# One stage of two dense graph layers, or two stages on neighbouring graphs

## The chip, the cores and the metric

The kernel runs on one core of one Trainium2 chip. The metric is the device time of one launch in microseconds; the figure for a kernel is the median of its runs. One execution is recorded by the hardware profiler.

The engines have short names in the profile: PE is TensorE (matmuls and transposes), DVE is VectorE, ACT is ScalarE, POOL is GpSimd, which here issues the indirect gathers, and SP issues nearly all other DMAs. Each engine works through its own list of instructions in order, and waits on semaphores for the others.

## The reference, cut to what matters

Sixteen graphs of 1024 nodes with 64 features each, an adjacency matrix of 1024 x 1024 floats per graph, and four layers, each of the form x + layer(relu(layernorm(x))):

```
h = max(layernorm(x), 0);  x = x + L0(h, adj)   # two-layer MLP, relu(A @ m), then a GRU cell
h = max(layernorm(x), 0);  x = x + L1(h, adj)   # (h * dinv) summed over neighbours, @ kernel, relu
h = max(layernorm(x), 0);  x = x + L2(h, adj)   # thin the neighbours, weighted quantiles of them, MLP
h = max(layernorm(x), 0);  x = x + L3(h, adj)   # (A + I) @ h, divided by the row sums
```

Layers 0, 1 and 3 multiply by the whole adjacency matrix. Layer 2 instead needs, for every node and feature, quantiles over that node's neighbours. The kernel makes lists of neighbours, gathers their rows of the table h and sorts them. The lists depend on the adjacency alone; the gathers need the table, which is the output of layers 0 and 1.

## The kernel before, in words

**Stages of a graph.** Lines 1852 to 1858 make, for every graph b, twelve Python generators: `fetch` and `load` (the adjacency is fetched, transposed on PE and stored as adjT in DRAM), `code`, `rank`, `cut` and `list` (the lists of neighbours, ending in the indices idxH and idxL), `mid` (layers 0 and 1 and the norm ahead of layer 2, dense01, line 1328), `gath` (POOL's gathers: 28 for the 128 nodes with the longest lists, "heavy", and 54 for all others, "light", in two groups), `sort` (heavy sorts on VectorE), `smalls` (light sorts), `sums`, and `rear` (the end of layer 2 and layer 3, dense23).

**What orders the work.** The program is not a loop. The class Order (line 209) keeps a model clock for each engine; `run` (line 241) resumes, again and again, the stage whose next piece can start earliest, and on a tie the one that stands first in the list of stages. What a stage issues when resumed goes at the end of its engines' instruction lists. The list is sorted by the dictionary `first` (line 1859): rear, sums and gath, then mid, list, cut, rank and code, then load and fetch, and the sorts last; within one rank by graph, so an older graph comes first. A stage can wait for another through `after(...)`: `middle` (line 1806) waits for mid of the graph before; `gathers` (line 1811) for its own list and its own mid, and for the last graph's gathers; `loads` (line 1768) for the rear stage DEPTH graphs back, since adjT, the table and other DRAM buffers exist DEPTH times (line 677).

**Buffers.** A tile name or tag has a number of buffers; a new tile with a tag waits, on the chip, for the readers of the old one. X, the running features of the graph in mid, has one buffer (line 1329), the norm's output hm has one, and the [128, 1024] tiles m1T, rz, g0 and g1 share the one buffer "big".

**Layer by layer in mid.** X is fetched; layernorm_relu (line 1226) takes a reduction on VectorE, eight squares with accumulation and a square root on ScalarE, three small VectorE steps, and eight scaled relus on ScalarE. The MLP follows (transposes, product, second product), then `propagated` (line 1288): sixteen matmuls of 512 columns against adjT, whose eight row blocks `streamed` (line 1275) brings in as tiles am of 512 KB, three buffers for all users. The stage that streams is put at the head of the list of stages. The GRU follows with sigmoid and tanh on ScalarE, and X is updated (line 1391, the instruction X<-X,hm). Then layer 1: row scales dinv, the norm into tr, the propagation, the product with wk, the transposition back and the scaling into u1, X updated again (X<-X,u), stored as x1 for the rear stage, normed once more (hm) and stored as the table tab (line 1422).

**Two PSUM pools** serve all stages: four tiles "bank" and two tiles "bank2"; a propagation holds a bank2 from its first matmul to its eviction.

Of the kernel before, what the change touches and what calls it, by code (L numbers as in the profile page):

```python
# [18 lines left out]
P = 128  # L19
EPS = 1e-5  # L20
STRIP = 1
DEPTH = 5
LIGHTBUFS = (2, 1)
HB = 2
SGN = 2
# [386 lines left out]
def kernel(  # L412
# [117 lines left out]
    def lists_for_all():  # L530
# [694 lines left out]

        def layernorm_relu(X, h=None, who="m", times=None):

            yield "V", X
            s = wp.tile([P, NT], F32, name="ln_s", bufs=2)
            V.reduce_sum(s, X, AX.X)  # L1230
            V.tensor_scalar(s, s, -1.0 / H, None, ALU.mult)
            yield "A", s
            v = wp.tile([P, NT], F32, name="ln_v", bufs=2)
            if h is None:
                h = wp.tile([P, NT, H], F32, name="h" + who, tag="h2r" if who == "r" else None, bufs=1)
            for t in range(NT):
                A.activation(h[:, t, :], X[:, t, :], AF.Square, bias=s[:, t : t + 1], accum_out=v[:, t : t + 1])
            A.activation(v, v, AF.Sqrt, bias=eps, scale=1.0 / H)
            yield "V", v
            V.reciprocal(v, v)  # L1240
            if times is not None:
                V.tensor_mul(v, v, times)
            V.tensor_mul(s, s, v)
            yield "A", s, v
            for t in range(NT):
                A.activation(h[:, t, :], X[:, t, :], AF.Relu, bias=s[:, t : t + 1], scale=v[:, t : t + 1])
            return h
# [6 lines left out]
        def t2(name, who="m"):  # L1254
            return wp.tile([P, NT, H], F32, name=name, tag="t2" + who, bufs=1)
# [69 lines left out]
                pm.append(q)  # L1325
            return pm

        def dense01(b, S):
            X = wp.tile([P, NT, H], F32, name="X", bufs=1)
            S_.dma_start(X, x[b].rearrange("(t p) h -> p t h", p=P))  # L1330

            h = yield from layernorm_relu(X)
            cat = wp.tile([P, N], F32, name="cat")
            yield from transposed(h, cat[0:H, :])
            yield "T", cat
            m1T = wp.tile([P, N], F32, name="m1T", tag="big")
            pm = yield from product(w1, cat[0:H])
            yield from evicted(pm, m1T[0:H], AF.Relu, b1)
            yield "T", m1T
            yield after(f"load{b}")  # L1340
            p2 = yield from bank()
            T.matmul(p2, *bias(0), start=True, stop=False)
            ams = streamed(b, 0)
            for t in range(NT):
                o = p2[:, t * H : (t + 1) * H]
                T.matmul(o, m1T[0:H, t * P : (t + 1) * P], w2, start=False, stop=t == NT - 1)
            yield "A", p2
            A.activation(m2x[:, :, 0:H], p2.rearrange("p (t h) -> p t h", h=H), AF.Relu)
            ps1.close(p2)
            pm = yield from propagated(b, m2x, 0, ams)  # L1350

            yield "A", pm
            A.copy(m1T[H : H + 1, :], pm[H : H + 1, :])
            yield from evicted(pm, cat[H:P], AF.Relu)
            yield "T", m1T
            pr = yield from bank()
            for t in range(NT):
                T.transpose(
                    pr[:, t : t + 1], m1T[H : H + 1, t * P : (t + 1) * P], ident[H : H + 1, H : H + 1]
                )  # L1360
            yield "V", pr
            S["rs"] = rs = st.tile([P, NT], F32, name="rs")
            V.tensor_scalar(rs, pr[:, 0:NT], 1.0, None, ALU.add)
            ps1.close(pr)
            rz = wp.tile([P, NT, 2 * H], F32, name="rz", tag="big")
            nn = t2("nn")
            for g in range(2):
                yield "T", cat
                pg = yield from bank2()
                for i in range(4):  # L1370
                    t = 4 * g + i
                    o = pg[:, i * 4 * H : (i + 1) * 4 * H]
                    if i % 2 == 0:
                        T.matmul(pg[:, i * 4 * H : (i + 2) * 4 * H], *bias(2), start=True, stop=False)
                    T.matmul(o, cat[:, t * P : (t + 1) * P], wg, start=False, stop=i % 2 == 1)
                pgv = pg.rearrange("p (i c) -> p i c", c=4 * H)
                gs = slice(4 * g, 4 * g + 4)
                yield "A", pg
                A.activation(rz[:, gs, :], pgv[:, :, 0 : 2 * H], AF.Sigmoid)
                yield "V", rz  # L1380
                V.tensor_mul(nn[:, gs, :], pgv[:, :, 2 * H : G], rz[:, gs, 0:H])
                V.tensor_add(nn[:, gs, :], nn[:, gs, :], pgv[:, :, G : 4 * H])
                ps2.close(pg)
            yield "A", nn
            A.activation(nn, nn, AF.Tanh)
            yield "V", nn

            V.tensor_sub(h, h, nn)
            V.tensor_mul(h, h, rz[:, :, H : 2 * H])
            V.tensor_add(h, h, nn)  # L1390
            V.tensor_add(X, X, h)

            ams = streamed(b, 1)

            dinv = wp.tile([P, NT], F32, name="dinv", bufs=2)
            V.tensor_scalar(dinv, rs, 1e-30, None, ALU.max)
            yield "A", dinv
            A.activation(dinv, dinv, AF.Sqrt)
            yield "V", dinv
            V.reciprocal(dinv, dinv)  # L1400
            V.scalar_tensor_tensor(dinv, rs, 0.0, dinv, ALU.is_gt, ALU.mult)
            tr = yield from layernorm_relu(X, t2("tr"), "m", dinv)
            pm = yield from propagated(b, tr, 1, ams, own=True)
            g0 = wp.tile([P, N], F32, name="g0", tag="big")
            yield from evicted(pm, g0[0:H])
            yield "T", g0
            pm = yield from product(wk, g0[0:H])
            g1 = wp.tile([P, N], F32, name="g1", tag="big")
            yield from evicted(pm, g1[0:H])
            pa = yield from back(g1[0:H])  # L1410
            yield "A", pa
            u1 = t2("u1")
            scaled(u1, pa, dinv, AF.Relu)
            ps1.close(pa)
            yield "V", u1
            V.tensor_add(X, X, u1)

            yield "S", X
            S_.dma_start(D[b % DEPTH]["x1"].rearrange("(t p) h -> p t h", p=P), X)
            h2 = yield from layernorm_relu(X)  # L1420
            yield "S", h2
            S_.dma_start(D[b % DEPTH]["tab"][1 : N + 1, :].rearrange("(t p) h -> p t h", p=P), h2)

# [75 lines left out]
        def sort_heavy(b, S):  # L1499
# [92 lines left out]
            yield ("V",)  # L1592

            agh = qp.tile([P, 64], F32, name="agh", bufs=2)
            split = qp.tile([P, 320], F32, name="split", bufs=1)
            pair = kept = 0
            for _, nr, q, bf, where in KEPT:
                n = nr // 4
                wv = wb[:, kept : kept + nr // 2 * q].rearrange("p (a i s) -> p a i s", i=2, s=q)
                v, k0 = None, 0  # L1600
                if len(where) > 1:
                    v = split[:, 0 : nr // 2 * q].rearrange("p (a s i) -> p a i s", i=2, s=q)
                for first, st_, k in where:
                    w = hb[bf]
                    ap = [list(z) for z in w.ap]
# [159 lines left out]
        def after(*names):  # L1765
            return lambda: all(n in order.done for n in names)
# [39 lines left out]
        def middle(b, S):  # L1806
            if b:
                yield after(f"mid{b - 1}")
            yield from dense01(b, S)

        def gathers(b, S):
            yield after(f"list{b}", f"mid{b}")
            if b:
                yield after(f"gath{b - 1}")
            if b >= HB:
                yield after(f"heavy{b - HB}")
            yield from gather_heavy(b, S)
            yield f"gh{b}"
            for g in range(len(NETS)):
                if b >= LIGHTBUFS[g]:  # L1820
                    yield after(f"sum{b - LIGHTBUFS[g]}.{g}")
                yield from gather_light(b, S, g)
                yield f"gl{b}.{g}"
# [28 lines left out]
        for b in range(B):  # L1852
            S = {}
            for name, stage in (
                ("rear", rear), ("mid", middle), ("fetch", fetching), ("load", loads), ("code", coding), ("rank", ranking), ("cut", cutting), ("list", listing),
                ("gath", gathers), ("sort", sorts), ("smalls", light_sorts), ("sums", sums),
            ):
                order.add(f"{name}{b}", stage(b, S))
        first = {"rear": 0, "sums": 0, "gath": 0, "conv": 1, "mid": 1, "list": 1, "cut": 1, "rank": 1, "code": 1, "load": 2, "fetch": 2, "sort": 7, "smalls": 7}
        order.stages.sort(key=lambda q: first[q[0].rstrip("0123456789")])  # L1860
        with tc.manual_schedule():
            order.run()
# [383 lines left out]
```

## Time and profile before

| what | us |
|---|---|
| median of three runs | 2694.49 |
| the three runs | 2689.75 to 2709.9 |
| the profiled execution | 2692.04 |
| its span, first to last instruction | 2690.2 |
| mean granted clock of TensorE | 0.769 of full |

How to read the profile: nearly every instruction carries the line L406, since the helper class Engine issues them all there; so instructions are told apart by the tiles that they write and read, "out<-in", with numbers left out. A row of a group reads: line, engine, operation, tiles, count, then busy time and mean length in ns, then the idle time of that engine just before these instructions and what ended most of it. A row of a timeline reads: start, length, engine, operation, tiles, count, and in brackets idle time before it and what ended it. A row of a view by stretches gives the stretch, its length, the busy time and instruction count of PE, its weight loads (PEld), DVE, ACT and POOL, the granted clock, and the busy share of the DMA engines with GB/s. A row of waits reads: who waited for whom, us in total, times, the longest.

### The profile page before, as it was taken

The numbers are of one execution on the slowest core, as the hardware profiler recorded it, in microseconds if no ns is written. First come the engines' busy times: TensorE is split into PE (matmuls) and PEld (weight loads), VectorE is DVE, ScalarE is ACT, GpSimd is POOL, SyncE is SP. The second block draws the span as 40 slices with busy tenths as digits, with TensorE's granted clock in tenths as the row PEclk, the third lists the DMA queues.
The fourth block names the chain that finished last, engine by engine and source line by source line (L and its number), as shares of the span: only waits on it lengthen the run. The fifth ranks groups of instructions, "written<-read, shape, count | busy, mean of one in ns | idle before, by whom it ended". The sixth has DMA issues, their size and how long they took to land.

```text
span 2690.2 us, 35021 instructions
## 1 busy us (share of the span) xinstructions
PE 1855.6 (69%) x9250; PEld 976.0 (36%) x9250; DVE 2034.3 (76%) x6403; ACT 1650.2 (61%) x5062; POOL 1590.3 (59%) x1502
## 2 busy tenths in 40 slices
PE   5866777678877667776777758688676757675314
PEld 3433444334343333434433334344333423232102
DVE  3448879986967969679893977979599694968581
ACT  8567876856575864778647676675767555353312
POOL 4037367776647674475746837476574745767761
PEclk7867787787868689686887859788686977877566
DMA  7546656565566556473656627475563644444322
GB/s 223 171 133 200 192 157 185 155 186 167 157 179 175 152 155 189 130 245 97 190 156 172 217 69 215 156 213 146 170 206 88 182 136 124 142 118 142 75 56 83
DMA packets 388338, 423.93 MB, mean 158 GB/s; under 512 B 160668, under 2 KB 297442, under 8 KB 388130
## 3 DMA queue, kind: packets, MB, share of 16 engines
q1 hardware_dynamic: 340610, 374.10, 44.1%
q0 software_dynamic: 47520, 47.51, 9.4%
q8 instruction: 76, 1.25, 0.2%
q14 instruction: 132, 1.08, 0.1%
HBM read 337.08 MB, written 84.37 MB: 157 GB/s over the span
## 4 chain that ended last, share of the span: by engine, by line
DVE 35%; PE 25%; ACT 15%; DMA 10%; POOL 6%; issue 5%; SPq 3%; DVEq 0%; ACTq 0%; POOLq 0%
PE bank L406 25%; DVE hb L406 12%; DMA am<-adjT 6%; DVE s L406 5%; POOL s L406 5%; DVE o L406 4%; SPq L406 3%; ACT sgn L406 2%; ACT hm L406 2%; DVE ln_s L406 1%; ACT u L406 1%; ACT s L406 1%; ACT junk L406 1%; DMA s<-tab,idxL 1%; ACT strip L406 1%
## 5 line engine op out<-in xcount | busy, mean ns | idle before, releaser
L406 POOL DMA_INDIRECT s<-tab,idxL x864 | 980.0, 1134 | 263.4 <-issue 257.9
L406 POOL DMA_INDIRECT gh<-tab,idxH x448 | 457.1, 1020 | 694.7 <-PE bank L406 174.8
L406 DVE TENSOR_TENSOR hb<-hb 128x128 f32<-128x128 f32 (+10 forms) x1040 | 520.9, 535 | 41.9 <-ACT hb L406 37.2
L406 PE MATMUL bank<-am,tr 128*64 128x512 f32 x512 | 281.7, 692 | 114.9 <-ACT tr L406 50.2
L406 PE MATMUL bank<-am,hr 128*64 128x512 f32 x512 | 265.2, 656 | 72.5 <-DMA am<-adjT 38.7
L406 PE MATMUL bank<-am,m2x 128*65 128x512 f32 x512 | 260.0, 648 | 35.4 <-DMA am<-adjT 34.2
L406 PE MATMUL bank<-ident,a 128*128 128x128 f32 x1024 | 192.2, 332 | 43.9 <-DMA a<-in_adj_dram 14.2
L406 ACT COPY strip<-bank 128x512 f32<-128x512 f32 x256 | 144.3, 586 | 90.5 <-PE bank L406 84.5
L406 ACT ACTIVATE s<-s,wl 128x64 f32<-128x64 f32 x704 | 188.6, 342 | 17.6 <-DVE s L406 17.6
L406 POOL DMA_INDIRECT zz<-agg,posi x128 | 125.6, 981 | 91.4 <-issue 37.0
L406 DVE TENSOR_TENSOR hb<-hb,hb 128x488 f32<-128x488 f32 (+7 forms) x368 | 173.2, 484 | 5.0
L406 PEld LDWEIGHTS bank<-am,tr 128*64 128x64 f32 x512 | 74.6, 157 | 277.1 <-issue 148.2
L406 PEld LDWEIGHTS bank<-ident,a 128*128 128x128 f32 x1024 | 141.0, 169 | 94.0 <-issue 29.8
L406 PE MATMUL bank<-cx,oh 128*128 128x133 f16 (+1 forms) x1280 | 144.1, 262 | 25.9 <-DVE oh L406 18.9
L406 ACT ACTIVATE g<-bank 64x512 f32<-64x512 f32 x96 | 51.9, 586 | 168.5 <-PE bank L406 168.5
L406 PEld LDWEIGHTS bank<-am,hr 128*64 128x64 f32 x512 | 70.0, 149 | 228.4 <-issue 135.1
L406 DVE TENSOR_TENSOR o<-s 128x1152 f32<-128x1152 f32 (+2 forms) x192 | 139.8, 751 | 17.1 <-DMA s<-tab,idxL 16.0
L406 ACT ACTIVATE sgn<-strip 128x1024 bf16<-128x1024 f32 x128 | 135.2, 1056 | 18.8 <-issue 9.6
L406 ACT ACTIVATE junk<-bank,nkey 128x1024 bf16<-128x1024 f32 x128 | 141.2, 1117 | 5.5 <-PE bank L406 5.5
L406 DVE TENSOR_TENSOR s<-s 128x128 f32<-128x128 f32 (+5 forms) x272 | 104.1, 398 | 52.9 <-ACT s L406 49.9
L406 DVE TENSOR_TENSOR s<-s,o 128x576 f32<-128x576 f32 (+5 forms) x256 | 138.0, 547 | 2.4
L406 ACT ACTIVATE sgn<-sgn 128x1024 bf16<-128x1024 bf16 x128 | 135.3, 1057 | 4.1
(399 smaller groups left out, 3986.0 us busy)
## 6 DMA issues: line engine op xcount, KB each, us to landing
am<-adjT SPq DMA_DIRECT2D x384, 512.0 KB
a<-in_adj_dram SPq DMA_DIRECT2D x128, 512.0 KB
adjT<-strip SPq DMA_DIRECT2D x128, 512.0 KB
s<-tab,idxL POOLq DMA_INDIRECT x864
gh<-tab,idxH POOLq DMA_INDIRECT x448
wb<-wd SPq DMA_DIRECT2D x32, 196.0 KB
X<-in_x_dram SPq DMA_DIRECT2D x16, 256.0 KB
x<-X SPq DMA_DIRECT2D x16, 256.0 KB
```

What stands on the lines that cost most here:

```text
L406: return f(*args, **kw)
```

## The change

dense01 is cut after the GRU. The first part, dense0, stays in the stage `mid`; the second, dense1, becomes a stage `next` with rank 1 in `first`, as mid has, and placed before mid of the same graph. `next` of graph b waits for mid of b and next of b-1; `mid` of graph b waits for mid of b-1 and for next of b-2; the gathers wait for next instead of mid. X gets two buffers. The second part gets its own buffers: tiles with the tag "t2n", h2 (before in the buffer of hm) among them, "bign" of 64 rows for g0 and g1, and ln_s and ln_v by stage. DEPTH goes from 5 to 6. The tile `split` (320 columns) that the heavy stage's weighting used is dropped; the front of the buffer hb[1] takes its place.

```
-DEPTH = 5
+DEPTH = 6
...
-            s = wp.tile([P, NT], F32, name="ln_s", bufs=2)
+            s = wp.tile([P, NT], F32, name="ln_s" + who, bufs=2)
...
-            v = wp.tile([P, NT], F32, name="ln_v", bufs=2)
+            v = wp.tile([P, NT], F32, name="ln_v" + who, bufs=2)
...
-        def dense01(b, S):
-            X = wp.tile([P, NT, H], F32, name="X", bufs=1)
+        def dense0(b, S):
+            S["X"] = X = wp.tile([P, NT, H], F32, name="X", bufs=2)
             S_.dma_start(X, x[b].rearrange("(t p) h -> p t h", p=P))
...
             V.tensor_add(X, X, h)
 
+        def dense1(b, S):
+            X, rs = S["X"], S["rs"]
             ams = streamed(b, 1)
...
-            tr = yield from layernorm_relu(X, t2("tr"), "m", dinv)
+            tr = yield from layernorm_relu(X, t2("tr", "n"), "n", dinv)
             pm = yield from propagated(b, tr, 1, ams, own=True)
-            g0 = wp.tile([P, N], F32, name="g0", tag="big")
-            yield from evicted(pm, g0[0:H])
+            g0 = wp.tile([H, N], F32, name="g0", tag="bign")
+            yield from evicted(pm, g0)
...
-            u1 = t2("u1")
+            u1 = t2("u1", "n")
...
-            h2 = yield from layernorm_relu(X)
+            h2 = yield from layernorm_relu(X, t2("h2", "n"), "n")
...
-            split = qp.tile([P, 320], F32, name="split", bufs=1)
...
-                    v = split[:, 0 : nr // 2 * q].rearrange("p (a s i) -> p a i s", i=2, s=q)
+                    v = hb[1][:, 0 : nr // 2 * q].rearrange("p (a s i) -> p a i s", i=2, s=q)
...
         def middle(b, S):
             if b:
                 yield after(f"mid{b - 1}")
-            yield from dense01(b, S)
+            if b >= 2:
+                yield after(f"next{b - 2}")
+            yield from dense0(b, S)
+
+        def second(b, S):
+            yield after(f"mid{b}")
+            if b:
+                yield after(f"next{b - 1}")
+            yield from dense1(b, S)
 
         def gathers(b, S):
-            yield after(f"list{b}", f"mid{b}")
+            yield after(f"list{b}", f"next{b}")
...
-                ("rear", rear), ("mid", middle), ("fetch", fetching), ("load", loads), ("code", coding), ...
+                ("rear", rear), ("next", second), ("mid", middle), ("fetch", fetching), ("load", loads), ("code", coding), ...
...
-        first = {"rear": 0, "sums": 0, "gath": 0, "conv": 1, "mid": 1, ...}
+        first = {"rear": 0, "sums": 0, "gath": 0, "next": 1, "mid": 1, ...}
```

More of the change, by code (lines that the diff above doesn't have):

```diff
@@ L1401, in dense01 @@
             V.scalar_tensor_tensor(dinv, rs, 0.0, dinv, ALU.is_gt, ALU.mult)
-            tr = yield from layernorm_relu(X, t2("tr"), "m", dinv)
+            tr = yield from layernorm_relu(X, t2("tr", "n"), "n", dinv)
             pm = yield from propagated(b, tr, 1, ams, own=True)
-            g0 = wp.tile([P, N], F32, name="g0", tag="big")
-            yield from evicted(pm, g0[0:H])
+            g0 = wp.tile([H, N], F32, name="g0", tag="bign")
+            yield from evicted(pm, g0)
             yield "T", g0
[L1407 to L1410, printed above, removed]
+            pm = yield from product(wk, g0)
+            g1 = wp.tile([H, N], F32, name="g1", tag="bign")
+            yield from evicted(pm, g1)
+            pa = yield from back(g1)
             yield "A", pa
-            u1 = t2("u1")
+            u1 = t2("u1", "n")
             scaled(u1, pa, dinv, AF.Relu)
@@ L1854, in lists_for_all @@
             for name, stage in (
-                ("rear", rear), ("mid", middle), ("fetch", fetching), ("load", loads), ("code", coding), ("rank", ranking), ("cut", cutting), ("list", listing),
+                ("rear", rear), ("next", second), ("mid", middle), ("fetch", fetching), ("load", loads), ("code", coding), ("rank", ranking), ("cut", cutting), ("list", listing),
                 ("gath", gathers), ("sort", sorts), ("smalls", light_sorts), ("sums", sums),
@@ L1858, in lists_for_all @@
                 order.add(f"{name}{b}", stage(b, S))
-        first = {"rear": 0, "sums": 0, "gath": 0, "conv": 1, "mid": 1, "list": 1, "cut": 1, "rank": 1, "code": 1, "load": 2, "fetch": 2, "sort": 7, "smalls": 7}
+        first = {"rear": 0, "sums": 0, "gath": 0, "next": 1, "mid": 1, "list": 1, "cut": 1, "rank": 1, "code": 1, "load": 2, "fetch": 2, "sort": 7, "smalls": 7}
         order.stages.sort(key=lambda q: first[q[0].rstrip("0123456789")])
```

## The prediction, made before the changed kernel ran

> **What bounds the kernel now.** I read the page first, for the load of the engines:
>
> ```profile
> span 2690.2 us, 35021 instructions
> ...
> PE 1855.6 (69%) x9250; PEld 976.0 (36%) x9250; DVE 2034.3 (76%) x6403; ACT 1650.2 (61%) x5062; POOL 1590.3 (59%) x1502
> ...
> L406 POOL DMA_INDIRECT gh<-tab,idxH x448 | 457.1, 1020 | 694.7 <-PE bank L406 174.8
> ```
>
> No engine is full, so something serial paces it. The timeline of SP's queue, where one graph's middle stage ends and the next begins (graphs 7/8, 8/9, 9/10):
>
> ```profile
> 1244.25 0.36 SPq L406 DMA_DIRECT2D tab<-hm  x1
> 1244.72 0.52 SPq L406 DMA_DIRECT2D X<-in_x_dram  x1
> ...
> 1404.09 0.36 SPq L406 DMA_DIRECT2D tab<-hm  x1
> 1404.56 0.52 SPq L406 DMA_DIRECT2D X<-in_x_dram  x1
> ...
> 1574.70 0.38 SPq L406 DMA_DIRECT2D tab<-hm  x1
> 1575.19 0.52 SPq L406 DMA_DIRECT2D X<-in_x_dram  x1
> ```
>
> The table of graph b is stored and X of graph b+1 is fetched 0.5 us later. In the trace this holds for every graph: dense01 never rests, and each takes 130 to 181 us. POOL can't gather graph b before its table is there:
>
> ```profile
> 1548.79 0.94 POOL L406 DMA_INDIRECT s<-tab,idxL  x1 [0.30 <-issue]
> 1577.83 0.95 POOL L406 DMA_INDIRECT gh<-tab,idxH  x1 [28.09 <-DMA tab<-hm]
> ```
>
> while the index list of that graph 9 was ready at 1422, 153 us earlier:
>
> ```profile
> 1422.03 0.19 DVE L406 CAST idxH<-bank 128x28 int32<-128x28 f16 x1 [2.52 <-PE bank L406]
> ```
>
> How much POOL loses so, from its own waits:
>
> ```profile
> POOL gh L406 <- PE bank L406: 174.8, 105, 6.2
> POOL gh L406 <- DVE nz L406: 128.8, 1, 128.8
> POOL gh L406 <- DMA tab<-hm: 104.2, 4, 31.9
> POOL gh L406 <- issue: 96.5, 315, 0.7
> POOL gh L406 <- DVE s L406: 69.9, 2, 43.5
> POOL gh L406 <- DVE idxH L406: 59.6, 2, 31.1
> ```
>
> Of 694.7 us before heavy gathers, 128.8 are the start, 174.8 waits for PE inside a graph (buffers gh), 96.5 issue. The other 294.6 are single gaps of 10 to 44 us between graphs; 59.6 of them (graphs 1 and 4) end with the list idxH, the others when the middle stage does, whatever the releaser named. So 235 us hang on dense01.
>
> Gathers of graph 4 start at 756 in the trace, those of graph 15 at 2493: a pace of 157.9 us per graph. The last gathers are followed by 192 us of gathering, sorting and rear work.
>
> **The change part by part.** *Two stages.* No compute instruction is added or removed; each graph still has its 16 + 16 matmuls of dense layers, norms and stores. What moves is when they may start. Graph 8's first part runs from the X fetch (1244.72) to the update of X by hm (1323.13 + 0.69 = 1323.8), 79 us; the second from there to 1404.09, 80 us. Dense0 of graph b+1 may now run beside dense1 of graph b, so the dense part allows a pace of 80 us instead of 159. Even stretched by half, to 120, it is below all that follows. The pace is then set by what is late next.
>
> *What is late next: two candidates.* First the chain of gathers (a graph's after the last one's): in the trace graphs 4 to 14 take 130 to 146 us from first heavy to last light gather, mean 136.5. It can't go below that. Second, VectorE. It has 2034.3 / 16 = 127.1 us of work per graph, 80.5% of 157.9. Its fill by stretches, each one middle stage (columns: stretch, length, PE, PEld, DVE, ACT, POOL, clock, DMA):
>
> ```profile
> 430.00:587.00 157.00, 117.34 (x561) 64.53 (x562) 144.14 (x436) 107.05 (x326) 122.14 (x104) 0.77 0.63 180
> 909.00:1090.00 181.00, 127.18 (x707) 69.65 (x708) 150.46 (x483) 118.70 (x357) 101.85 (x90) 0.77 0.56 164
> 1245.00:1404.00 159.00, 121.94 (x638) 64.42 (x639) 142.13 (x454) 95.69 (x314) 95.99 (x90) 0.78 0.52 154
> ```
>
> That is 92%, 83% and 89%. Sorts have the last turn among ready stages and are VectorE's work, and light buffers come free only when they are summed; a VectorE that falls behind therefore stops the gathers too. I take 89%, the middle one: 127.1 / 0.89 = 142.8 us. That exceeds 136.5, so it sets the pace. Gain: 11 x (157.9 - 142.8) = 166 us, of the 235 that are there.
>
> *The start.* Gathers of graphs 0 to 4 begin at 162, 312, 452, 590 and 756; the lists idxH are ready at 162, 312, 444, 564 and 755. The first two and the fifth wait for lists, which the change doesn't touch: 0. Bounds: 25 us of gain (graph 3) against 30 of loss, a list gap more, if dense work takes turns from lists.
>
> *Transfers.* A graph still streams 24 am tiles of 512 KB through 3 buffers. Alone, graph 8's first eight took 24 us (1277 to 1301); with the rear's eight, sixteen took 49 (1333 to 1382): 3.05 us each, 73 per graph, under 142.8. New is a third stream, and each opens ahead of its norm: dense1's three tiles lie about 10 us unused (X at 1323.8, first matmul 1332.9), as they do now. Behind a waiting am issue in SP's queue stand the x1 and tab stores, which gathers wait for. PE now idles 112 us for am (34 + 39 + 39 in its three groups), 7 per graph. Bounds: nothing more, or as much again, 77 over 11 graphs, if it fell on the path; I take 0, since the dense stages have 60 us of slack, and keep 77 for the range.
>
> *Table loads of ScalarE.* Sigmoid and tanh of one graph now fall between square roots of another:
>
> ```profile
> 1310.66 1.28 ACT L406 ACT_TABLE_LOAD   x1
> 1311.96 0.60 ACT L406 ACTIVATE rz<-bank 128x512 f32<-128x512 f32 x1
> ```
>
> There are 38 (2.4 per graph), 1.30 us each up to the next instruction. The three activations of the gates can be parted twice: at most 4 loads more, 5.2 us per graph, on an engine with 1650.2 / 16 = 103 us of 142.8. Hidden: 0; without that cover 11 x 5.2 = 57 us. The Trainium skill (ScalarE: Activation LUTs, "What ACT_TABLE_LOAD costs" and "Table sets") speaks against the change: batch activations by set, since a switch takes 1.28 us and a drain of 1.38 besides. The trace shows the first and, in this place, 0.02 us for the second. By the page an estimate of 4 x 2.66 = 10.6 us per graph, 117 in all if bare, and still 0 under the cover.
>
> *The rest.* DEPTH 6 makes two more little DMAs on POOL (0.5 us each) inside its 128.8 us idle at the start: 0. A load waits for the rear stage six graphs back, not five: graph 5's went from its release at 598 to its output at 1234, 636 us, less than 5 x 142.8 = 714, so five would have sufficed: 0. The tile split becomes part of hb[1], same 32 multiplies, same engine and order: 0. Second X, bign and t2n remove waits inside a stage that no longer paces: 0.
>
> *Sum.* The profiled execution took 2692.0 us (span 2690.2 and 1.8 around); the median of the runs is 2694.5. 2692 - 166 = 2526; on the median's scale 2528, said as 2530.
>
> **The rivals.** *The gathers' floor.* VectorE fills further, the gaps close entirely: 2692 - 235 = 2457. For: 92% in one stretch, and 127.1 / 136.5 is 93%. Against: that stretch stands alone. Gathers also slow down when VectorE is busy: of neighbouring light gathers in the trace, pairs with VectorE's two-input operations in under 5% of the time between lie 1.26 us apart, with over 90%, 1.48 (DMA traffic was higher there too, so this doesn't isolate it). 90 gathers per graph at 1.48, and 174.8 / 16 = 10.9 of waits for PE, make 144 us: 2692 - 11 x 13.9 = 2539. The Trainium skill (GPSIMD Engine Reference, "Key points") states it: POOL shares its SBUF interfaces with VectorE and contends with two-input instructions. By that rule the time is about 2540 and the floor out of reach; the trace leans its way.
>
> *Contention, not the serial stage, is the pace.* Middle stages took 130 to 142 us in the first two and last two graphs, where less ran beside them, and about 160 between; so part of their length is queueing for engines, and that queue stays. VectorE was filled to 82% from 430 to 1404 (804.5 of 974 us in the view by stretches); if late transfers and waits in the engines' fixed orders keep it there, the pace is 127.1 / 0.82 = 155: 2692 - 11 x 2.9 = 2660.
>
> *Slower: the lists become the bound.* Two dense stages rank ahead of the lists of later graphs and both take turns. From graph 3 to 4 a list took 191 us (564 to 755), and the gathers waited for it; 0 to 4 took 148 each. At 165 per list the end is 756 + 11 x 165 + 192 = 2763, + 2: 2765. It decides from a pace of 158 on. Against: from graph 4 to 9 lists came 133 us apart (755 to 1422), under the same engines.
>
> *Nothing happens* would be a stage still serial; the conditions at the stages' heads exclude it, unless am buffers chain them: then 2695.
>
> **How the numbers follow.** Forecast (2470 to 2600) 0.50; floor 0.09; contention (2600 to 2700) 0.24; slower 0.15; nothing 0.02. The range 2450 to 2700 takes the floor and contention, leaving out 0.17 above and a little below. A measurement tells about 1% from no change. Under 2667.5: 0.50 + 0.09 + 0.13 of contention = 0.72. Within 1%: the other 0.11 and 0.02, less 0.01 to slower: 0.12. Slower 0.16.
>
> **What would show it.** Right: X of graph b+1 fetched some 80 us before the table of b; heavy gathers' idle down from 694.7 to about 530; VectorE near 81% of the span and 89% between 600 and 2200; gathers 143 us apart. Contention: gaps moved, VectorE still at 82%. Slower: gathers waiting for idxH each time. Wrong altogether: am waits of PE well over 112 us with the table stores late.

## The result, and the profile after

| | before | after |
|---|---|---|
| median of 12 runs, us | 2694.99 | 2673.07 |
| the runs, us | 2685.95 to 2709.9 | 2662.54 to 2680.45 |
| span of the profiled execution, us | 2690.2 | 2675.8 |
| start of the gathers of graph 4 and of graph 15 | 756, 2493 | 776, 2475 |
| pace between them, us per graph | 157.9 | 154.4 |
| from there to the end of the span | 197 | 201 |

The ratio is 0.9912, 95% interval 0.989 to 0.9933: faster by 0.9%, where 6% were forecast. The spans add up, in unrounded values: the start costs 20.2 us, eleven graphs at 3.51 give back 38.7, the tail costs 4.1; that is 14.4 less.

(Two other chips took 3742 and 3697 us for the kernel before; the runs made there, e1 to e4 on the first and m1 and m2 on the second, are set only against the kernel before on the same chip.)

The page of the kernel after, its engines and the rows that the prediction spoke of:

```profile
span 2675.8 us, 34997 instructions
...
PE 1893.6 (71%) x9250; PEld 983.2 (37%) x9250; DVE 2015.2 (75%) x6403; ACT 1644.5 (61%) x5060; POOL 1608.3 (60%) x1504
...
L406 POOL DMA_INDIRECT gh<-tab,idxH x448 | 477.7, 1066 | 666.8 <-PE bank L406 222.0
...
L406 PE MATMUL bank<-am,hr 128*64 128x512 f32 x512 | 279.7, 692 | 82.0 <-DMA am<-adjT 61.0
...
L406 PE MATMUL bank<-am,tr 128*64 128x512 f32 x512 | 278.3, 682 | 79.1 <-DMA am<-adjT 41.0
...
L406 PE MATMUL bank<-am,m2x 128*65 128x512 f32 x512 | 274.4, 677 | 50.4 <-DMA am<-adjT 49.9
```

POOL's idle time before heavy gathers fell by 28 us, from 694.7 to 666.8, where 165 were forecast; VectorE did not get fuller. Yet the two stages do run side by side. The timeline of SP's queue around graph 9:

```profile
1252.78 0.54 SPq L406 DMA_DIRECT2D X<-in_x_dram  x1
...
1395.49 0.43 SPq L406 DMA_DIRECT2D X<-in_x_dram  x1
...
1451.28 0.36 SPq L406 DMA_DIRECT2D x<-X  x1
...
1464.20 0.36 SPq L406 DMA_DIRECT2D tab<-h  x1
```

X of graph 9 is fetched at 1252.78, and X of graph 10 at 1395.49, 69 us before the table of graph 9 is stored at 1464.20. In the kernel before, the fetch came after the store. The table was then not needed for 90 us. The timeline of VectorE and POOL where graph 9's gathers start:

```profile
1553.85 0.18 DVE L406 CAST idxH<-bank 128x28 int32<-128x28 f16 x1
...
1554.31 0.94 POOL L406 DMA_INDIRECT gh<-tab,idxH  x1 [14.19 <-DVE dinv L406]
```

The list idxH of graph 9 is made at 1553.85 and the gathers start 0.5 us later. (The bracket names another VectorE result; the time shows that it is idxH.) This holds for the kernel: in 11 of 16 graphs the gathers start within 2 us of their list, where it was 3 of 16 before; averaged over graphs 4 to 15 the list is ready 10 us ahead of the gathers (before: 103), and x1, stored shortly before the table, 99 us ahead (before: 13). The two inputs of the gathers have changed places. POOL's waits say the same:

```profile
POOL gh L406 <- PE bank L406: 222.0, 86, 20.3
POOL gh L406 <- DMA adjT<-strip: 146.3, 1, 146.3
POOL gh L406 <- DVE idxH L406: 133.2, 6, 44.3
POOL gh L406 <- issue: 100.6, 330, 0.3
POOL gh L406 <- DVE dinv L406: 37.3, 2, 23.2
```

The row "DMA tab<-hm" (104.2 before) has no successor among them; idxH went from 59.6 to 133.2. The list itself is the end of a chain of stages (load, code, rank, cut, list). The first, load, may start only after the load of the graph before; its steps on ScalarE, around the ends of the loads of graphs 8 and 9:

```profile
1190.66 1.06 ACT L406 ACTIVATE sgn<-sgn 128x1024 bf16<-128x1024 bf16 x1
...
1199.62 1.06 ACT L406 ACTIVATE sgn<-strip 128x1024 bf16<-128x1024 f32 x1
...
1320.78 1.06 ACT L406 ACTIVATE sgn<-sgn 128x1024 bf16<-128x1024 bf16 x1
...
1327.12 1.06 ACT L406 ACTIVATE sgn<-strip 128x1024 bf16<-128x1024 f32 x1
```

Graph 8's load ends at 1191, graph 9's runs from 1200 to 1322, graph 10's starts at 1327. In 9 of the 11 graphs 5 to 15 the pause between loads is 15 us or less (before: 2 of 11). A load takes 140 us from its first to its last such step, on the mean of graphs 4 to 15, against 108 before. So load now hardly rests: of the eleven pauses only two are longer, 25 and 42 us.

### The profile page after: what moved, and what is told of

The parts are those of the page before. It is cut to its first block, busy times and chain, and to the rows that moved or that the text cites. A ratio compares the mean times of both kernels' runs of the same rounds, so it can differ in the third digit from the quotient of the medians.

```text
span 2675.8 us, 34997 instructions
## 1 busy us (share of the span) xinstructions
PE 1893.6 (71%) x9250; PEld 983.2 (37%) x9250; DVE 2015.2 (75%) x6403; ACT 1644.5 (61%) x5060; POOL 1608.3 (60%) x1504
## 4 chain that ended last, share of the span: by engine, by line
DVE 32%; PE 23%; ACT 13%; DMA 12%; POOL 9%; issue 6%; SPq 3%; DVEq 0%; ACTq 0%; POOLq 0%
PE bank L406 23%; DVE hb L406 13%; POOL s L406 7%; DMA am<-adjT 7%; DVE s L406 3%; SPq L406 3%; DVE o L406 3%; ACT s L406 2%; POOL gh L406 2%; ACT sgn L406 2%; ACT h L406 2%; DMA gh<-tab,idxH 1%; DMA s<-tab,idxL 1%; DMA adjT<-strip 1%; DVE oh L406 1%
## 5 line engine op out<-in xcount | busy, mean ns | idle before, releaser
L406 POOL DMA_INDIRECT s<-tab,idxL x864 | 965.8, 1118 | 263.4 <-issue 256.1
L406 POOL DMA_INDIRECT gh<-tab,idxH x448 | 477.7, 1066 | 666.8 <-PE bank L406 222.0
L406 PE MATMUL bank<-am,hr 128*64 128x512 f32 x512 | 279.7, 692 | 82.0 <-DMA am<-adjT 61.0
L406 PE MATMUL bank<-am,m2x 128*65 128x512 f32 x512 | 274.4, 677 | 50.4 <-DMA am<-adjT 49.9
L406 POOL DMA_INDIRECT zz<-agg,posi x128 | 136.2, 1064 | 87.3 <-issue 32.9
L406 PE MATMUL bank<-cx,oh 128*128 128x133 f16 (+1 forms) x1280 | 151.5, 274 | 7.0 <-DVE oh L406 6.1
L406 ACT ACTIVATE sgn<-strip 128x1024 bf16<-128x1024 f32 x128 | 135.3, 1057 | 20.2 <-PE bank L406 17.0
L406 PEld LDWEIGHTS bank<-am,m2x 128*65 128x65 f32 x512 | 72.3, 155 | 204.8 <-issue 130.9
```

Source lines behind the costliest of these rows:

```text
L406: return f(*args, **kw)
```

## The experiments

The theory after the result: the next serial stage behind dense01 is the making of the lists, above all load, which dense work of later graphs, ranked ahead of it, slows down. The rivals: the gathers still wait for the dense stages; contention for engines as such is the pace; or DEPTH 6 or the new buffers cost what the split gains.

**Does anything still wait for the table?** The kernels e3 and f2 (one edit, on two chips) and e4 and f3 let graph b gather from the table of graph b-1; all work is still done.

```
-                out=dst, out_offset=None, in_=D[b % DEPTH]["tab"][:, :],
+                out=dst, out_offset=None, in_=D[max(b - 1, 0) % DEPTH]["tab"][:, :],
...
-            yield after(f"list{b}", f"next{b}")
+            yield after(f"list{b}", f"next{max(b - 1, 0)}")
```

(In the kernel before it is mid in place of next.)

> The changed kernel, with the gathers of a graph reading the table of the graph before (a changed computation) and waiting for that graph's dense1 instead of their own. Theory L and theory C: the table is there some 100 us before the lists already, so 2673 within 1%. If dense stages still hold up gathers: faster by 1% or more.

> The kernel of e3 again. Each engine has the same instructions in the same order as in the changed kernel; the only difference is that gathers read the table of the graph before, written one graph earlier. Theories L and C: 2673 within 1%, since the table is not what gathers wait for. If dense stages still hold up gathers: 2645 or less.

e3: 3541.09 against 3741.5, 0.9494 (0.942 to 0.9568). f2: 2667.96 against 2690.65, 0.9928 (0.9903 to 0.9953). The changed kernel's own ratio is 0.9912 (0.989 to 0.9933): taking the wait away gains nothing. The table is not what its gathers wait for.

> The kernel before, with the same loosening: gathers of a graph read the table of the graph before (a changed computation) and wait for that graph's dense01. It takes away the wait that the prediction priced at 235 us and leaves dense01 one serial stage. The prediction's reading: 2460 to 2560, unless dense01 itself keeps the pace through the rear stage. Theory L: the lists are next in line at a pace near 154, 2660 to 2690. Theory C gives the same, 2650 to 2690.

> The kernel of e4 again: dense01 stays one serial stage, gathers read the table of the graph before. The prediction's reading (235 us hang on the wait for dense01): 2460 to 2560. Theory L (the lists stand right behind, at 154 per graph): 2655 to 2690. Theory C: the same.

e4: 3661.44 against 3741.5, 0.9773 (0.9686 to 0.986). f3: 2649.57, 0.983 (0.9797 to 0.9863). In the kernel before, with dense01 whole, the wait was worth 41 us, not 235, and a little more than theory L gave it. POOL's waits in f3:

```profile
POOL gh L406 <- DVE nz L406: 164.3, 2, 134.0
POOL gh L406 <- DVE idxH L406: 139.3, 6, 34.2
POOL gh L406 <- PE bank L406: 132.7, 79, 6.9
POOL gh L406 <- issue: 100.7, 329, 0.7
```

The idle time that was booked to the table is now booked to the list: idxH 59.6 has become 139.3, and in 12 of 16 graphs the gathers start within 2 us of it. That the lists lay 103 us ahead before did not mean that they could go faster: their pace without the wait is 155.5 us per graph, and a load takes 133 us where it took 108.

**Do dense turns slow the lists?** Both dense stages are ranked behind the list stages (e1 and f1, one kernel), or only the first part (g2):

```
-        first = {..., "next": 1, "mid": 1, "list": 1, ...}
+        first = {..., "next": 2, "mid": 2, "list": 1, ...}      # e1, f1
+        first = {..., "next": 1, "mid": 2, "list": 1, ...}      # g2
```

> The changed kernel with one edit: the two dense stages have rank 2 instead of 1, behind code, rank, cut and list. Theory L (the list chain is the bound of the changed kernel, and it is held up because two dense stages take their turns ahead of it): lists come sooner, the pace of the gathers falls from 154.5 us per graph to about 143 to 148, time 2540 to 2610. Theory C (engines shared by all stages hold VectorE at about 80% in any order): the pace stays, 2650 to 2690, or above that because the dense stages now come late.

> The kernel of e1 again, for a chip on which the kernel before takes its usual 2695. Theory L (lists are the bound and are held up by the two dense stages ranked ahead of them): gathers about 143 to 148 us apart, 2540 to 2610. Theory C (shared engines hold VectorE at 80% in any order): 2650 to 2690.

e1: 3612.27 against 3741.5, 0.966 (0.9579 to 0.974), no more than e3 gained there, whose kernel equals the kernel after on the other chip: on that chip the rank showed nothing. Its trace says why in part: in the first ten graphs the gathers start within 6 us of the store of their table, and 403.4 us of POOL's waits end with it, so there the dense stages, put behind, were what came late. f1: 2552.16 against 2690.65, 0.949 (0.9449 to 0.9531), 121 us less than the changed kernel. The gathers are 143.1 us apart. Ranks of 1.5 in place of 2 give every engine the same order of instructions, so what counts is the order of dense stages against list stages, not against load, which has rank 2 too. Half of the effect is there early: the list of graph 4 is ready at 636 (708 in the kernel after), that of graph 15 at 2328 (2473), and over these graphs the lists lie 54 us ahead of the gathers on the mean. Yet from graph 5 on the lists of f1 come hardly faster: 153.9 us apart up to graph 15, against 154.6 in the kernel after. What f1 has is a lead, 138 us at graph 5 (790 in place of 928), and by graph 15 the gathers have caught up with the lists to within 5 us. In seven of the first nine graphs (0, 2 to 5, 7 and 8) its gathers start within 5 us of the store of their table, so dense work holds them there again. With lists 153.9 us apart, 143.1 is not a pace that f1 could keep.

> The changed kernel with only the first dense part (mid) at rank 2; the second (next), which the gathers wait for, keeps rank 1. Theory L: half of the turns that dense work takes from the lists are given back, 2570 to 2630, between f1 (2552) and the changed kernel (2673). If it is the second part's turns that hold up the lists: 2660 to 2680.

g2: 2544.49 against 2694.76, 0.9463 (0.9425 to 0.95), better than expected: the first part alone, put behind, gives as much as both. Its row of heavy gathers:

```profile
L406 POOL DMA_INDIRECT gh<-tab,idxH x448 | 473.3, 1057 | 494.0 <-PE bank L406 177.9
```

POOL's idle time is down to 494.0, the table is still not late (x1 lies 73 us ahead), and the lists and the gathers both come 145.5 us apart. Here the lists themselves are faster, 145.2 from graph 5 to 15 too.

**Is it the rank, or when the first part runs?** h1 leaves the ranks alone and lets the first part of graph b wait for the rank stage of its own list:

```
         def middle(b, S):
+            yield after(f"rank{b}")
```

> The changed kernel with all ranks as they are; mid of a graph waits, besides, for the rank stage of its own graph, so the first dense part can't start ahead of that graph's lists. Theory L, as sharpened by g2 (the first dense part of later graphs takes turns long before anyone needs it): the lists get them, 2540 to 2600. If the gain of g2 came from something else that its ranks change: about 2673.

h1: 2545.41 against 2694.86, 0.9437 (0.9406 to 0.9469), the same as g2 by another road; lists and gathers 146 us apart. Both roads hold the first part back, and both speed up the lists.

> The kernel of g2, with gathers that read the table of the graph before (a changed computation); every engine keeps its order. If lists, gathers and VectorE set the pace by now: 2544 within 1%. If the dense stages, now behind the lists, have become what the gathers wait for: 2515 or less.

h2 is g2 with f2's edit (graph b gathers from the table of graph b-1): 2542.59, 0.9443 (0.941 to 0.9477), the same as g2. Nor does the table bind there.

**Would the rank alone have done it?** g1 is the kernel before with `"mid": 2`.

> The kernel before (one serial dense01 per graph) with its stage mid at rank 2, behind the list stages. Theory L, with the serial stage as the bound of the kernel before: lists come early and wait, dense01 gets longer than its 158 us since it gives way, 2750 to 2850. If the rank alone brings the gain of f1, and the two stages are not needed: 2550 to 2620.

g1: 2825.99 against 2694.76, 1.0516 (1.047 to 1.0561), slower. POOL's waits:

```profile
POOL gh L406 <- DMA tab<-hm: 446.7, 11, 132.3
POOL gh L406 <- PE bank L406: 205.8, 96, 24.8
```

With dense01 whole and last in turn, its tables come late and no list does (219 us and more ahead from graph 3 on); a load takes 80 us there, where it took 108 in the kernel before. So the split is needed for the gain, and the rank as well: neither does it alone.

**DEPTH.** e2 and g3 are the kernel after with `DEPTH = 5`.

> The changed kernel with DEPTH 5 as before. Both theories: the loads of a graph start long after the rear stage that releases them, so no difference, 2673 within 1%. If the sixth graph in flight is what brought the small gain: 2690 to 2710.

> The kernel of e2 again (the changed kernel with DEPTH 5). Both theories: 2673 within 1%, the sixth graph in flight is not used. If it carries the small gain: about 2695.

e2: 3578.81 against 3741.5, its runs between 3497 and 3597; too wide for an interval. g3: 2665.39 against 2694.76, 0.9904 (0.9872 to 0.9936), the same as the kernel after. DEPTH 6 shows no effect.

**Is load the stage that binds?** Load and code hand the signs of the adjacency to each other through two buffers sgn. k1 gives them a third; the room for it comes from DEPTH 5, from a constant and from the second buffers of four small tiles, of which the diff shows drT (cum, mra and LC go the same way). m1 was meant as the control: the same without the third.

```
-DEPTH = 6
+DEPTH = 5
-SGN = 2
+SGN = 3              # k1 alone
-    offdiagh = const.tile([P, P], F16, name="offdiagh")
...
-            drT = ap_.tile([2 * NT, P], F16, name="drT", bufs=2)
+            drT = ap_.tile([2 * NT, P], F16, name="drT", bufs=1)
...
```

> The changed kernel with three sgn buffers in the load stage in place of two; the space comes from DEPTH 5, an unused constant and second buffers of four small tiles (mra, cum, LC, drT). Theory M (the load stage, one graph after the other and back to back, 140 us each with its pauses, is the serial stage that sets 154 per graph): load of a graph shortens, 2590 to 2635. If load only follows a pace set elsewhere: 2665 to 2680.

> The control to k1: the changed kernel with the space freed (DEPTH 5, an unused constant gone, one buffer for mra, cum, LC and drT), but two sgn buffers. Theory M: 2660 to 2685, as the changed kernel. If the freed buffers themselves made the gain of k1: about 2577.

k1: 2577.35 against 2694.01, 0.9586 (0.9537 to 0.9636), more than expected. A load takes 120 us in place of 140, the gathers start 59 us earlier (graph 4 at 717) and come 150.6 us apart. m1: 3524.19 against 3697.0, 0.9521 (0.9438 to 0.9603). That does not serve as a control: k1's ratio lies inside the interval of m1, the kernel after was not run on that chip, and the trimming alone changes the plan (in the trace of m1, ScalarE departs from the changed kernel's order after 350 of some 5060 instructions; in that of g3, with DEPTH 5 alone, it keeps that order to the end). A load takes 186 us in m1 and 188 in e2 and e3, which keep the changed kernel's order on ScalarE but ran on the other slower chip; so the trimming does not seem to shorten loads by itself, but the third buffer's share of k1 is not isolated.

k2 takes one of the two ScalarE steps out of each tile of load. The relu ahead of the sign is left out. m2 does so in the kernel before.

```
-                A.activation(sgn, strip[:, :, o : o + P], AF.Relu)
-                A.activation(sgn, sgn, AF.Sign)
+                A.activation(sgn, strip[:, :, o : o + P], AF.Sign)
```

> The changed kernel with sgn made by one ScalarE instruction (sign) in place of two (relu, then sign), which is the same for an adjacency without negative entries. It takes 8 x 1.06 us of ScalarE out of each load, 135 us in all. Theory M: the pace falls by 8 us or more, 2560 to 2600. If load is not the bound, ScalarE being 61% busy: 2655 to 2675.

> The kernel before with the one sign step of k2. There dense01 is the serial stage that paces, not load: if shortening load only helps where load is the bound, 2670 to 2700. If dense01 is itself long because it queues for ScalarE behind such work, it shortens too: 2580 to 2650.

k2: 2539.68, 0.9427 (0.9407 to 0.9447), 133 us below the kernel after and more than expected, for 128 instructions of 1.06 us: 8.5 us per graph of ScalarE's time, and a pace 9.3 shorter (145.1 against 154.4). The pace fell by about the length of the step. But the loads themselves still take 140 us, so this does not say where in the chain it was gained, and ScalarE also lost 8% of its work. m2: 3543.13 against 3697.0, 0.9578 (0.9501 to 0.9655): the kernel before gains by it too, on that slower chip, with its lists 140 us ahead of the gathers and x1 16. So a gain from this edit does not show that load was the bound.

k4 gives load and fetch rank 1, level with the dense stages:

```
-        first = {..., "load": 2, "fetch": 2, ...}
+        first = {..., "load": 1, "fetch": 1, ...}
```

> The changed kernel with load and fetch at rank 1, level with the list stages and the dense stages. Theory M: load gets turns that dense work of later graphs took, 2610 to 2650. If the list stages behind load are what suffers from the dense work: 2665 to 2690, since they lose turns to load too.

k4: 2597.12 against 2694.01, 0.9633 (0.9609 to 0.9657), more than expected: a load takes 128 us, the lists come 147 apart.

**Together.** k3 is g2 and k2 in one: `"mid": 2` and the single sign step.

> The edit of g2 (first dense part at rank 2) and the edit of k2 together. Theory M: both act on the same stage, the pace falls towards the 136 us of the chain of gathers and VectorE's 127, 2470 to 2520. If g2 already reached what the engines allow: 2530 to 2550.

k3: 2471.99 against 2694.01, 0.9178 (0.9155 to 0.9201), the fastest of all. Its page:

```profile
span 2465.5 us, 34882 instructions
...
PE 1815.3 (74%) x9250; PEld 950.1 (39%) x9250; DVE 2012.0 (82%) x6403; ACT 1507.8 (61%) x4930; POOL 1618.7 (66%) x1504
...
L406 POOL DMA_INDIRECT gh<-tab,idxH x448 | 482.7, 1077 | 451.4 <-PE bank L406 130.8
```

and the stretch from 600 to 2200 (stretch, length, PE, PEld, DVE, ACT, POOL, clock, DMA share, GB/s), of k3:

```profile
600.00:2200.00 1600.00, 1241.54 (x6288) 640.89 (x6288) 1386.53 (x4340) 1031.79 (x3420) 1111.52 (x1003) 0.83 0.63 179
```

against the kernel after:

```profile
600.00:2200.00 1600.00, 1199.07 (x5918) 613.78 (x5916) 1272.43 (x4021) 1060.99 (x3263) 1006.41 (x918) 0.80 0.59 172
```

VectorE is at 1386.53 / 1600 = 87% in k3, at 80% in the kernel after. In k3 the lists lie 32 to 109 us ahead from graph 4 to 11, and x1 45 us on the mean. In 9 of the 15 graphs behind the first, the gathers start 0.3 us after those of the graph before have ended: there the chain of gathers itself is the bound. In graphs 5, 7, 9 and 10 they start 3 to 5 us after the store of their table: the first dense part, at rank 2, is the later input again. The two gains (129 of g2 and 133 of k2, from the kernel after) add up to 201 only.

## Why the prediction was wrong in its size, point by point

*What bounds the kernel now.* Half right. dense01 was serial and never rested. But "235 us hang on dense01" failed: without the wait for the table the kernel before gains 41 us (f3). The 235 were read as what the gathers would win if tables came at once; they were only what the later of two inputs was booked for. The other one, the list, lay 103 us ahead on the mean, but kept a pace of 155.5 when the table no longer held the gathers.

*What is late next.* This is the step that failed. It named two candidates, the chain of gathers and VectorE, and took 142.8 us per graph; the third, the lists, stood among the rivals, and was set aside because lists 4 to 9 came 133 us apart. The lists became the bound, at 154.4; in no graph of the changed kernel do the gathers wait for the table: in 11 they start within 2 us of their list, in the other five as soon as the gathers of the graph before have ended. The trace of before could not have given that number by itself: its loads started 154.4 us apart from graph 4 to 15 as well, but each took 108 of them and rested 47, and a stage that is held back takes about the pace of the whole (157.9 there); that the two agree need not mean more. How long a load takes depends on what goes ahead of it: 80 us in g1, 133 in f3, 140 in the changed kernel. The term for VectorE was also too high. 92, 83 and 89% are three of the four fullest of the eleven middle stages between 430 and 2211 us, whose shares run from 73 to 92% with a median of 81%; with 81% the same sum gives 157 us per graph and next to no gain. The kernel after has 80%. A pace like the forecast's was not out of reach: g2 came to 145.5, and k3 to 143.6 with VectorE at 87%; but no run shows that VectorE set the pace there, and in k3 the chain of gathers did in most graphs.

*The slower rival* had the mechanism as far as the runs show one: dense work ranked ahead of the lists of later graphs takes turns from them, and the lists become what the gathers wait for (g2 and h1 give the turns back). That it takes two dense stages is not shown, since f3 keeps its lists at 155.5 with one. Its price was 165 us per list, measured 154.6 from list 5 to list 15; it was to decide from 158 on, and so it ended as a small gain in place of a loss. Its sum used 192 us for the tail, which is 197 from the start of the last graph's gathers. Its chance of 0.15 was too low, since the case against it rested on the six lists of graphs 4 to 9, 133 us apart; from 4 to 15 the same trace has 149.8. *Contention* gave 2660, near the time measured, and a VectorE stuck at about 82% (it is 80%); but not by contention alone: a change of rank (g2) lifts it to 85% and a pace of 145.5 with the same work.

*The start*: 20 us lost, inside the bounds of -25 and +30, in the way named there: the list of graph 3 is ready at 623 in place of 564, graph 3's gathers end at 776, and graph 4's start with that.

*Transfers*: PE's waits for am went from 112 to 152 us (61.0 + 41.0 + 49.9). That is 2.5 us per graph, on a stage that is done 99 us before it is needed: 0 on the path, as taken.

*Table loads*: 0 was right, and the fear behind the bound was not borne out; the group of ScalarE in the kernel after:

```profile
L406 ACT ACT_TABLE_LOAD x36 | 46.2, 1283 | 12.0 <-PE bank L406 7.8 <-DMA X<-in_x_dram 3.7
```

There are 36 loads, two fewer than before, at 1.28 us each. The Trainium skill (ScalarE: Activation LUTs, "What ACT_TABLE_LOAD costs") has that 1.28, and the trace agrees; the interleaving of two graphs, which by its rule could have multiplied them, did not.

*DEPTH 6* at 0 was right (g3). *The split tile, second X, bign and t2n* at 0: no run tried them by themselves; the kernels that reach 143 to 146 us per graph all have them.

*The gathers' floor* (2457, or 2540 by slower gathers): k3 lies at 2472. One heavy gather takes 1077 ns there, 1066 in the kernel after and 1020 before, and a graph's chain of gathers, from first start to last end, 136.5, 141.4 and 136.6 us. The Trainium skill (GPSIMD Engine Reference, "Key points") has POOL contend with VectorE's two-input instructions; the 6% on one gather fits that but does not isolate it. The chain of k3 was no longer than before, so the estimate of 2540 was not a floor.

*What stays open.* Whether load was held up in the turns of ScalarE and TensorE or for its two sgn buffers: k1 (a buffer), k2 (ScalarE's work) and k4 (its rank) each gave 76 to 133 us, and no run parts them. A plan in which only the second part is put back wasn't tried. Nor is it excluded that the plan of the kernel after was an unlucky one: f1, g2, h1, k1, k2 and k4 each also change the order of the whole program, f2 and g3, which gain nothing over the kernel after, keep ScalarE's order of it, and no run changes the order without favouring lists or load. Against chance speak g2 and h1, which free the lists by two roads and come within 1 us of each other.

## What to carry to other kernels

Before a serial stage is split, find the next serial one and its pace without the first: an experiment that only takes the wait away (f3) shows at once how much there is to win with the rest of the plan as it is, here 41 us and not 235. That a stage lies 100 us ahead, or rests for a third of its time, says little of how fast it can go: it rests because it is held back, and it stretches when others get its turns. And where a stage stops being the bound, look at its priority again: the split was worth 0.9% with the old rank and 5.4% with the new, and the new rank without the split cost 5.2%.

## What the runs showed of the hardware that was not expected

The granted clock of TensorE was higher the fuller TensorE was kept: 0.759 of full at a busy share of 67% (g1), 0.769 at 69% (before), 0.778 at 71% (after), 0.80 at 72% (g2) and 0.813 at 74% (k3). Which of the two follows the other no run separates. The busy time of the same 9250 matmuls does not simply follow the clock: 1882.8 us in g1, 1855.6 in before, 1893.6 in after, 1835.1 in g2 and 1815.3 in k3. So how much of a gain is due to the clock stays open.
